# Decays in numbers of their own per slot, inputs scaled by a table of leads, and new tables for a four-layer image kernel

## The chip, the cores and the metric

The kernel runs on one core of one Trainium2 chip. The metric is device time in microseconds (us), from start to end of one execution. Times of a core's five engines are told apart: TensorE (PE, with its weight loads as PEld), VectorE (DVE), ScalarE (ACT), GpSimd (POOL), and SyncE (SP), which here only issues DMAs.

## The reference

The input is 32 images of 128 channels by 32 x 32 pixels, float32. Four layers are applied, each as `x = x + layer(group_norm(x))`:

1. a 3 x 3 convolution;
2. a 1 x 1 convolution, then a selective scan (Mamba) over the 1,024 pixels in four orders (forward and back, channels as they are and flipped), summed, and a second 1 x 1 convolution;
3. a gate of means over rows and columns, with two shorter selective scans;
4. a small simulated circuit on every pixel.

Nearly all time is layer 2. For each image and each of its four directions there are 256 inner channels (two halves `h` of 128) and 16 states `n`, and each state of each half is a recurrence along the 1,024 pixels:

```python
dA = jnp.exp(dt_t[..., None] * A)
h = dA * h + (dt_t * u_t)[..., None] * B_t[:, None, :]
y = jnp.einsum('bdn,bn->bd', h, C_t)
```

## The kernel before

Channels lie on the 128 partitions, pixels along the free dimension. The scans run in **slots**: one slot is one step `i`, that is one state `n` of one half `h` of one direction (`Direction`). A direction has 32 slots, an image 128, and the 32 images 4,096; layer 3 adds 64 more. `Steps.run` writes the instructions of slot `i` in one fixed order, and each engine works through its own queue in the order in which they were written; semaphores make it wait for data and for free buffers.

A step needs four things, made by different engines:

- the **decay** `da` (line 781): ScalarE's exponential of `dt` scaled by `A`, 128 x 1024. Before, slot `i` makes the decay of step `i + 3`;
- the **input** `bu`, 128 x 1024 in PSUM, made in one of two ways. A *plain* input: TensorE spreads row `B` over the partitions with two 512-column bf16 matmuls (line 802, in `spread`), and VectorE multiplies it by `du` in place (line 826, `input`). A *turned* input: `du` stands transposed in `dut`, pixels on the partitions, so that `B` is one number per partition; eight scalings of 128 x 128 write `but` (ScalarE, line 818, or as one instruction on GpSimd, line 815), and eight transposes on TensorE (line 795) bring it back into `bu`. `TURNED` says which of a direction's 32 slots are turned, `POOLED` which of these GpSimd scales;
- the **scan** (line 834): VectorE's `tensor_tensor_scan` over `da` and `bu`, into `hh`;
- the **weighing** (line 843): GpSimd multiplies `hh` by row `C`, spread over the partitions by a DMA (`cc`, line 772). Eight transposes on TensorE (line 879) then add it up in PSUM (`y`), and after 16 states ScalarE reads the sum (`evict`, line 898).

Before, slot `i` writes: `evict`, decay `i + 3`, ScalarE's waiting reads of PSUM (`flush`), `spread(i + 1)`, `scan(i)`, `input(i + 1)`, more reads, stages of other work, scaling of input `i + 4`, weighing `i`, sum of `i - 2`, load of `cc` for `i + 3`, and again stages.

The *stages* are all that is not the recurrence: convolutions (line 1131), projections (line 373: `uc`; 394, 485, 581), gates, transposes, statistics, the ways out. Where each stands is written in `PLACES`: for every kind of stage a slot relative to the direction's first, and a place within it (-1 is behind the slot's own work). `Table` carries this out. ScalarE reads the projections with silu and softplus, which need other activation tables than the decays' exponential: `Kernel.activation` (line 921) notes which table is in, a load is put ahead of it where the table changes, and `exps` (line 926) loads the exponential's table again before the next decay.

`Work.BUFS` gives the number of buffers in each ring of tiles. PSUM has two buffers for `bu`, two for all stages' matmuls (`mm`), and the sums `y`.

Of the kernel before, what the change touches and what calls it, by code (L numbers as in the profile page):

```python
# [41 lines left out]


TURNED = (
# [4 lines left out]
)  # L49

POOLED = (
    (5, 11, 21, 27),
    (7, 8, 13, 23, 24),
    (5, 12, 18, 22, 31),
    (7, 15, 19, 25),
)


# [1 line left out]
PLACES = {  # L60
    0: {
        "first": [
            (-41, -1), (-41, -1), (-38, -1), (-38, -1), (-35, 2), (-34, 0), (-32, 1), (-31, 2),
            (-28, 3), (-26, 3), (-25, 0), (-24, 2), (-23, 2), (-22, 3), (-18, 3), (-5, 2),
            (-3, 3), (-2, 2),
        ],
        "second": [
            (-8, 2), (-1, 0), (2, -1), (8, 1),
        ],
    },  # L70
    1: {
        "first": [
            (-48, 3), (-47, 3), (-46, 3), (-44, -1), (-39, 3), (-39, 3), (-38, 2), (-37, 2),
            (-33, 2), (-32, -1), (-31, -1), (-30, -1), (-29, 1), (-27, 0), (-25, 1), (-23, -1),
            (-13, 0), (-4, 0),
        ],
        "second": [
            (5, 3), (6, 2), (8, 3), (10, -1),
        ],
        "gates": [  # L80
            (1, -1), (3, 1), (6, -1), (17, -1),
        ],
        "back": [
            (21, 3), (26, 2),
        ],
        "out": [
            (39, -1), (47, 0), (52, -1), (54, 2),
        ],
    },
    2: {  # L90
        "first": [
            (-53, 2), (-52, 2), (-51, 1), (-48, 2), (-42, 0), (-40, -1), (-39, 3), (-37, 2),
            (-34, 2), (-33, 1), (-32, 0), (-31, 3), (-29, 3), (-28, 1), (-26, 1), (-15, 2),
            (-6, 3), (-1, -1),
        ],
        "second": [
            (-4, 2), (1, 2), (3, 2), (5, -1),
        ],
    },
    3: {  # L100
        "first": [
            (-53, 2), (-53, 2), (-51, 0), (-49, 1), (-45, 2), (-45, 3), (-44, 1), (-44, 3),
            (-40, 2), (-39, 3), (-36, 0), (-27, 1), (-23, 0), (-20, 1), (-18, -1), (-9, 3),
            (-8, 1), (-4, 2),
        ],
        "second": [
            (-15, -1), (-7, -1), (1, -1), (12, 0),
        ],
        "gates": [
            (-7, 2), (9, 1), (12, 0), (13, 0),  # L110
        ],
        "back": [
            (22, 3), (31, 3),
        ],
        "out": [
            (37, 2), (40, 3), (42, 1), (50, 3),
        ],
    },
    "layer0": [
        (-79, 3), (-76, 2), (-75, 2), (-73, -1), (-69, 0), (-64, 3), (-63, 2), (-62, 3),  # L120
        (-55, 3), (-54, -1), (-51, 1), (-50, 0), (-49, 2), (-47, 2), (-46, 0), (-43, 3),
        (-42, 0),
    ],
    "end": [
        (60, 3), (61, 3), (63, 1), (66, 0), (68, 0), (76, 2), (81, 3), (86, 1), (94, -1),
    ],
}


def constants():  # L130
# [565 lines left out]
class Steps:  # L696
# [3 lines left out]
    SLOTS = 2 * DS  # L700
# [3 lines left out]
        self.cc, self.da, self.hh, self.bu, self.but = {}, {}, {}, {}, {}  # L704
        self.sums = self.owed = None

    def run(self, ways, plan):

        k = self.k
        steps = [(w, h, n) for w in ways for h in range(2) for n in range(DS)]  # L710
        self.steps = steps
        for i in range(3):
            self.load(i)
        for i in range(3):
            self.decay(i)
# [55 lines left out]
        self.cc[i] = t = k.work.tile([P, w.T], F32, tag="cc", name="cc")  # L771
        k.nc.sync.dma_start(t, w.rows[n : n + 1].to_broadcast([P, w.T]))

    def decay(self, i):
        if not self.has(i):
            return
        k, (w, h, n) = self.k, self.steps[i]
        assert ("dt", h) in w.made
        self.da[i] = t = k.work.tile([P, w.T], F32, tag="da", name="da")
        k.exps()  # L780
        k.nc.scalar.activation(t, w.dt[h], AF.Exp, scale=w.m.na[:, h, n : n + 1])  # L781
        if w.segment:

            k.nc.gpsimd.memset(t[:, 0 :: w.segment], 0.0)
# [16 lines left out]
        for cs in w.chunks:  # L801
            k.nc.tensor.matmul(t[:, cs], k.sel[:, n], w.parts[:, cs], start=True, stop=True)  # L802

    def scale(self, i, engine):

        if not self.has(i) or not self.turned(i):
            return
        if (engine is self.k.nc.gpsimd) != self.pooled(i):
            return
        k, (w, h, n) = self.k, self.steps[i]  # L810
        assert "bt" in w.made and all(("dut", h, g) in w.made for g in range(w.T // P // 4))
        self.but[i] = t = k.work.tile([P, w.T // P, P], F32, tag="but", name="but")
        if self.pooled(i):
            each = w.bt[:, :, n : n + 1].to_broadcast([P, w.T // P, P])
            engine.tensor_tensor(t, w.dut[h], each, ALU.mult)  # L815
            return
        for b in range(w.T // P):
            engine.activation(t[:, b], w.dut[h][:, b], AF.Copy, scale=w.bt[:, b, n : n + 1])  # L818
# [82 lines left out]
class Kernel:  # L901
# [175 lines left out]
    def images(self):  # L1077
        tc, nc, d = self.tc, self.nc, self.d
        with ExitStack() as ctx:
# [179 lines left out]
            images, ways, plan = [], [], Table(self)  # L1259
# [460 lines left out]
```

## Time and profile before

| what | value |
|---|---|
| time, median of 3 runs | 12,785.62 us (12,782.69 to 12,790.93) |
| the profiled execution | 12,796.0 us, span 12,794.2 us |
| granted TensorE clock, mean | 0.983 |
| decays, line 781 | 4,096, mean 1,144 ns |
| scans, line 834 | 4,160, mean 2,274 ns |
| plain inputs' products, line 826 | 1,856, mean 1,212 ns |
| scalings of turned inputs on ScalarE, line 818 | 13,824, mean 392 ns |
| the same on GpSimd, line 815 | 576, mean 1,919 ns |
| table loads, lines 921 and 926 | 695 and 683, mean 1,283 ns |
| weighing, line 843 | 4,160, mean 2,373 ns |

A group's busy time is the union of its instructions' times, its mean the length of a single one; where instructions of an engine overlap in its pipeline, the mean is longer than the distance from one start to the next. The idle time of an engine is put down to the instruction that ended it. The 64 decays of layer 3 read other tiles and stand in groups of their own.

### The profile page before, as it was taken

Reading aid. Unit: us, or ns where it says so; the run is one execution under the profiler, and the core shown is the slowest. Engines: PE = TensorE matmul, PEld = TensorE weight load, DVE = VectorE, ACT = ScalarE, POOL = GpSimd, SP = SyncE. Lnnn points to the kernel's source line nnn. Section 1 sums busy time; section 2 is a strip of 40 time slices with the busy share of each in tenths; the row PEclk is TensorE's granted clock in tenths of the full one; section 3 lists DMA queues with packets and bytes.
Section 4 is the critical chain, followed back from the end, with each engine's and each line's share of the span. In section 5 each row is a group of like instructions: output and inputs, shape, how many; then the busy total and the mean of one; then the engine's idle time right before and its main releaser. Section 6 shows DMA issues by size and latency. Waiting matters only on the chain.

```text
span 12794.2 us, 209849 instructions
## 1 busy us (share of the span) xinstructions
PE 12351.5 (97%) x75694; PEld 8583.8 (67%) x75694; DVE 12186.0 (95%) x7817; ACT 12115.8 (95%) x22601; POOL 12040.9 (94%) x6421
## 2 busy tenths in 40 slices
PE   8999999999999999999999999999999999999888
PEld 5676676666666666766666666676666666667542
DVE  7999999999999999999999999999999999999876
ACT  7999999999999999999999999999999999999843
POOL 6999999999999999999999999999999999999865
PEclk9999999999999999999999999999999999999978
DMA  4555555555555555555555555555555555555432
GB/s 138 183 185 180 184 184 185 182 185 183 181 184 184 186 184 181 184 182 186 183 186 184 181 184 183 185 181 186 184 184 181 184 184 184 183 185 184 168 118 94
DMA packets 633943, 2278.38 MB, mean 178 GB/s; under 512 B 77480, under 2 KB 81144, under 8 KB 632776
## 3 DMA queue, kind: packets, MB, share of 16 engines
q1 hardware_dynamic: 630600, 2263.06, 50.9%
q8 instruction: 599, 9.81, 0.3%
q14 instruction: 440, 3.60, 0.1%
q10 hardware_dynamic: 2304, 1.90, 0.0%
HBM read 2221.35 MB, written 43.33 MB: 177 GB/s over the span
## 4 chain that ended last, share of the span: by engine, by line
PE 46%; ACT 39%; DVE 7%; issue 4%; POOL 3%; DMA 1%; DVEq 0%; SPq 0%; POOLq 0%; ACTq 0%
ACT da L781 14%; PE y L879 13%; ACT but L818 13%; PE mm L373 8%; PE bu L795 7%; DVE hh L834 5%; PE bu L802 4%; PE mm L1131 3%; ACT L926 3%; ACT L921 3%; POOL hh L843 2%; PE mm L394 2%; PE y L858 2%; PE mm L485 1%; DVE bu L826 1%
## 5 line engine op out<-in xcount | busy, mean ns | idle before, releaser
L843 POOL TENSOR_TENSOR hh<-hh,cc 128x1024 f32<-128x1024 f32 x4160 | 9768.1, 2373 | 371.2 <-DVE hh L834 188.8
L834 DVE TENSOR_TENSOR_SCAN hh<-da,bu 128x1024 f32<-128x1024 f32 x4160 | 9303.9, 2274 | 315.6 <-PE bu L795 55.3
L879 PEld LDWEIGHTS y<-cbig,hh 128*128 128x128 f32 x33280 | 3776.6, 142 | 1273.0 <-issue 977.6
L781 ACT ACTIVATE da<-dt,m_na 128x1024 f32<-128x1024 f32 x4096 | 4568.8, 1144 | 28.1 <-DVE hh L834 19.6
L879 PE MATMUL y<-cbig,hh 128*128 128x128 f32 x33280 | 4400.9, 276 | 71.7 <-POOL hh L843 67.2
L818 ACT ACTIVATE but<-dut,bt 128x128 f32<-128x128 f32 x13824 | 4216.4, 392 | 30.1 <-PE bu L795 30.1
L795 PE MATMUL bu<-cbig,but 128*128 128x128 f32 x18432 | 2413.6, 274 | 131.2 <-DVE hh L834 93.5
L826 DVE TENSOR_TENSOR bu<-du,bu 128x1024 f32<-128x1024 f32 x1856 | 2250.0, 1212 | 102.6 <-PE bu L802 91.9
L795 PEld LDWEIGHTS bu<-cbig,but 128*128 128x128 f32 x18432 | 2072.3, 141 | 323.9 <-issue 144.0
L373 PE MATMUL mm<-hpad,m_wc 128*128 128x512 f32 x4096 | 1937.2, 603 | 5.0 <-ACT dt L921 0.8
L373 PEld LDWEIGHTS mm<-hpad,m_wc 128*128 128x128 f32 x4096 | 712.2, 190 | 760.6 <-issue 688.5
L802 PE MATMUL bu<-parts,sel 48*128 48x512 bf16 x3712 | 1133.6, 386 | 64.8 <-DVE hh L834 55.4
L815 POOL TENSOR_TENSOR but<-dut,bt 128x1024 f32<-128x1024 f32 x576 | 1105.2, 1919 | 0.0
L921 ACT ACT_TABLE_LOAD x695 | 891.7, 1283 | 13.7 <-DMA my_zw<-in_my_zw 1.4
L926 ACT ACT_TABLE_LOAD x683 | 876.3, 1283 | 15.6 <-DMA cbig<-in_cbig 3.6
L501 POOL TENSOR_TENSOR du<-dt,uc 128x1024 f32<-128x1024 f32 x260 | 616.2, 2370 | 18.4 <-ACT dt L921 18.4
L858 PEld LDWEIGHTS y<-m_skip,uc 128*128 128x128 f32 x4096 | 488.5, 193 | 101.1 <-issue 55.4
L1131 PE MATMUL mm<-xpad,w 128*128 128x512 f32 x1152 | 542.9, 608 | 2.7 <-ACT xpad L1116 2.7
L802 PEld LDWEIGHTS <-sel 48*128 48x128 bf16 x3712 | 211.6, 94 | 489.4 <-issue 303.0
L858 PE MATMUL y<-m_skip,uc 128*128 128x128 f32 x4096 | 516.5, 280 | 0.5 <-ACT back L898 0.3
L394 PE MATMUL mm<-uc,m_xw 128*128 128x512 f32 x1024 | 494.7, 606 | 7.4 <-ACT dut L530 7.4
L921 ACT ACTIVATE uc<-mm,m_pv 128x512 f32<-128x512 f32 x512 | 335.0, 686 | 54.5 <-PE mm L373 47.3
(207 smaller groups left out, 7380.5 us busy)
## 6 DMA issues: line engine op xcount, KB each, us to landing
cc<-rows SPq DMA_DIRECT2D x4160, 512.0 KB, 3.9
xt<-in_x SPq DMA_DIRECT2D x32, 512.0 KB, 5.8
x<-xt SPq DMA_DIRECT2D x32, 512.0 KB, 3.3
xt<-x SPq DMA_DIRECT2D x32, 512.0 KB, 3.9
out<-xt SPq DMA_DIRECT2D x32, 512.0 KB, 2.9
rows<-dbl SPq DMA_DIRECT2D x130, 64.0 KB, 4.5
stats<-st SPq DMA_DIRECT2D x32, 36.0 KB, 3.0
means<-stats SPq DMA_DIRECT2D x1, 1152.0 KB
```

The source lines that it names most:

```text
L373: nc.tensor.matmul(self.view(ps), m.wc[:, v, j, h * P : (h + 1) * P], self.taps(j, c), start=(j == 0), stop=(j == 3),)
L781: k.nc.scalar.activation(t, w.dt[h], AF.Exp, scale=w.m.na[:, h, n : n + 1])
L795: k.nc.tensor.matmul(t[:, b * P : (b + 1) * P], but[:, b], k.ident, start=True, stop=True, is_transpose=True,)
L802: k.nc.tensor.matmul(t[:, cs], k.sel[:, n], w.parts[:, cs], start=True, stop=True)
L818: engine.activation(t[:, b], w.dut[h][:, b], AF.Copy, scale=w.bt[:, b, n : n + 1])
L826: k.nc.vector.tensor_tensor(t, w.du[h], t, ALU.mult)
L834: k.nc.vector.tensor_tensor_scan(way(t), way(self.da.pop(i)), way(self.bu.pop(i)), 0.0, ALU.mult, ALU.add)
L843: k.nc.gpsimd.tensor_tensor(t, t, self.cc.pop(i), ALU.mult)
L858: nc.tensor.matmul(self.y[g][: w.bl, b], w.uc[h][:, at], m.skip[:, h], start=(b == 0), stop=False)
L879: k.nc.tensor.matmul(self.y[g][: w.bl, b], t[:, at], k.ident, start=False, stop=(n == DS - 1 and b == w.per - 1), is_transpose=True,)
L921: self.nc.scalar.activation(*args, **kw)
L926: self.nc.scalar.preload_act_table_set("natural_log_exp_and_others")
```

## The change

- **Decays.** `decay` no longer takes a step's number. It makes the next decay in line, and a new table `DECAYS` of 128 numbers says how many decays each slot of an image writes: 0, 1, 2 or 3. Three are made before the first slot, as before.
- **Scaling.** A turned input is no longer scaled four slots ahead of its step, but as many as the new table `LEADS` says for it, 2 to 7 (0 stands for plain inputs). `scale` looks from slot `i` at the steps up to eight ahead and scales those whose lead fits, first ScalarE's, then, after the weighing, GpSimd's.
- **Rings.** `da` has six buffers instead of five, `but` four instead of three.
- **Kinds of inputs.** `TURNED` has 75 entries in place of 72, `POOLED` 17 in place of 18.
- **Slots.** All numbers in `PLACES` are others; the stages are the same.

Layer 3 runs with one decay a slot and a lead of four throughout (the defaults of `run`).

```diff
--- before.py
+++ after.py
@@ -42,17 +42,17 @@
 
 
 TURNED = (
-    (4, 5, 6, 8, 9, 11, 13, 15, 16, 17, 19, 21, 22, 23, 25, 27, 28, 30),
-    (1, 2, 4, 7, 8, 10, 11, 13, 15, 16, 18, 22, 23, 24, 26, 28, 29, 30, 31),
-    (4, 5, 6, 7, 8, 11, 12, 13, 15, 16, 17, 18, 21, 22, 26, 28, 30, 31),
-    (1, 3, 5, 7, 8, 10, 11, 13, 15, 19, 21, 22, 23, 25, 29, 30, 31),
+    (2, 3, 5, 7, 9, 11, 12, 14, 16, 17, 19, 20, 22, 23, 25, 27, 29, 31),
+    (0, 2, 5, 7, 9, 11, 12, 13, 14, 16, 17, 18, 22, 23, 25, 27, 28, 29, 30, 31),
+    (4, 5, 6, 7, 8, 9, 11, 14, 15, 16, 18, 20, 21, 23, 24, 27, 30, 31),
+    (0, 2, 3, 6, 7, 9, 11, 12, 13, 14, 19, 20, 21, 22, 24, 27, 29, 30, 31),
 )
 
 POOLED = (
-    (5, 11, 21, 27),
-    (7, 8, 13, 23, 24),
-    (5, 12, 18, 22, 31),
-    (7, 15, 19, 25),
+    (7, 14, 23, 29),
+    (2, 12, 17, 22, 29),
+    (4, 15, 31),
+    (6, 9, 20, 21, 30),
 )
 
 
...
@@ -60,71 +60,94 @@
 PLACES = {
     0: {
         "first": [
-            (-41, -1), (-41, -1), (-38, -1), (-38, -1), (-35, 2), (-34, 0), (-32, 1), (-31, 2),
+            (-39, 1), (-39, 2), (-37, 3), (-36, -1), (-33, 2), (-31, -1), (-28, 0), (-28, 2),
...
+DECAYS = (
+    0, 1, 0, 1, 3, 0, 0, 1, 1, 2, 1, 2, 0, 0, 2, 1, 1, 1, 1, 2, 0, 2, 1, 1, 0, 2, 1, 1, 0, 0, 2, 2,
+    1, 0, 0, 0, 2, 2, 0, 1, 0, 2, 1, 1, 1, 1, 1, 3, 0, 0, 0, 2, 3, 0, 1, 0, 0, 2, 3, 0, 3, 0, 0, 2,
+    1, 2, 1, 0, 0, 1, 1, 0, 0, 1, 3, 3, 0, 1, 3, 1, 0, 2, 0, 0, 1, 0, 2, 0, 1, 2, 0, 1, 3, 0, 0, 1,
+    2, 0, 2, 0, 2, 3, 0, 0, 0, 0, 2, 1, 0, 2, 3, 0, 3, 0, 0, 0, 1, 2, 0, 0, 3, 1, 2, 1, 0, 2, 0, 1,
+)
+
+LEADS = (
+    (
+        0, 0, 2, 3, 0, 5, 0, 5, 0, 5, 0, 7, 5, 0, 7, 0, 5, 6, 0, 5, 5, 0, 3, 6, 0, 3, 0, 5, 0, 7, 0, 4,
+    ),
+    (
+        5, 0, 7, 0, 0, 5, 0, 7, 0, 4, 0, 5, 6, 4, 2, 0, 4, 7, 3, 0, 0, 0, 5, 7, 0, 6, 0, 7, 6, 6, 4, 4,
+    ),
+    (
+        0, 0, 0, 0, 5, 5, 6, 5, 5, 3, 0, 5, 0, 0, 5, 4, 3, 0, 5, 0, 7, 3, 0, 4, 6, 0, 0, 2, 0, 0, 5, 5,
+    ),
+    (
+        6, 0, 3, 2, 0, 0, 7, 5, 0, 7, 0, 3, 7, 5, 3, 0, 0, 0, 0, 4, 6, 4, 5, 0, 2, 0, 0, 7, 0, 2, 4, 4,
+    ),
+)
 
 
 def constants():
@@ -254,8 +277,8 @@
 
 
     BUFS = {
-        "uc": 4, "dt": 3, "du": 3, "dut": 2, "parts": 2, "dbl": 2, "cc": 3, "da": 5, "hh": 4,
-        "bt": 2, "but": 3,
+        "uc": 4, "dt": 3, "du": 3, "dut": 2, "parts": 2, "dbl": 2, "cc": 3, "da": 6, "hh": 4,
+        "bt": 2, "but": 4,
     }
 
     def __init__(self, pool):
@@ -704,20 +727,24 @@
         self.cc, self.da, self.hh, self.bu, self.but = {}, {}, {}, {}, {}
         self.sums = self.owed = None
 
-    def run(self, ways, plan):
+    def run(self, ways, plan, decays=(1,), leads=((4,) * SLOTS,)):
+
+
 
         k = self.k
+        self.leads, self.next = leads, 0
         steps = [(w, h, n) for w in ways for h in range(2) for n in range(DS)]
         self.steps = steps
         for i in range(3):
             self.load(i)
         for i in range(3):
-            self.decay(i)
+            self.decay()
         self.spread(0)
         self.input(0)
         for i in range(len(steps) + 2):
             self.evict()
-            self.decay(i + 3)
+            for _ in range(decays[i % len(decays)]):
+                self.decay()
             k.flush(False, vector=False)
             self.spread(i + 1)
             self.catch_up()
@@ -726,9 +753,9 @@
             k.flush(False)
             if self.has(i):
                 plan.slot(i, self.load_of(i))
-            self.scale(i + 4, k.nc.scalar)
+            self.scale(i, k.nc.scalar)
             self.weigh(i)
-            self.scale(i + 4, k.nc.gpsimd)
+            self.scale(i, k.nc.gpsimd)
             self.add(i - 2)
             self.load(i + 3)
             if self.has(i):
@@ -771,7 +798,9 @@
         self.cc[i] = t = k.work.tile([P, w.T], F32, tag="cc", name="cc")
         k.nc.sync.dma_start(t, w.rows[n : n + 1].to_broadcast([P, w.T]))
 
-    def decay(self, i):
+    def decay(self):
+
+        i, self.next = self.next, self.next + 1
         if not self.has(i):
             return
         k, (w, h, n) = self.k, self.steps[i]
@@ -801,12 +830,16 @@
         for cs in w.chunks:
             k.nc.tensor.matmul(t[:, cs], k.sel[:, n], w.parts[:, cs], start=True, stop=True)
 
-    def scale(self, i, engine):
-
-        if not self.has(i) or not self.turned(i):
-            return
-        if (engine is self.k.nc.gpsimd) != self.pooled(i):
-            return
+    def scale(self, slot, engine):
+
+        for i in range(slot + 1, slot + 9):
+            if not self.has(i) or not self.turned(i):
+                continue
+            lead = self.leads[i // self.SLOTS % len(self.leads)][i % self.SLOTS]
+            if i - slot == lead and (engine is self.k.nc.gpsimd) == self.pooled(i):
+                self.scaled(i, engine)
+
+    def scaled(self, i, engine):
         k, (w, h, n) = self.k, self.steps[i]
         assert "bt" in w.made and all(("dut", h, g) in w.made for g in range(w.T // P // 4))
         self.but[i] = t = k.work.tile([P, w.T // P, P], F32, tag="but", name="but")
@@ -1297,7 +1330,7 @@
                 plan.alone(PLACES[0]["first"][0][0])
                 self.circuit(Slices(self.work.tile([P, 2 * HW], F32, tag="carry", name="small")))
                 plan.alone(0)
-                Steps(self).run(ways, plan)
+                Steps(self).run(ways, plan, DECAYS, LEADS)
                 plan.alone()
```

More of the change, by code (lines that the diff above doesn't have):

```diff
@@ L62 @@
         "first": [
[L63 to L65 removed]
+            (-39, 1), (-39, 2), (-37, 3), (-36, -1), (-33, 2), (-31, -1), (-28, 0), (-28, 2),
+            (-24, 2), (-22, 3), (-21, 0), (-20, 3), (-18, 0), (-15, 2), (-11, 2), (-9, 3),
+            (-4, 3), (-3, 0),
         ],
         "second": [
[L68 removed]
+            (-10, 0), (0, 1), (3, 1), (6, 0),
         ],
@@ L72 @@
         "first": [
-            (-48, 3), (-47, 3), (-46, 3), (-44, -1), (-39, 3), (-39, 3), (-38, 2), (-37, 2),
-            (-33, 2), (-32, -1), (-31, -1), (-30, -1), (-29, 1), (-27, 0), (-25, 1), (-23, -1),
-            (-13, 0), (-4, 0),
+            (-50, 1), (-50, 3), (-49, -1), (-48, 3), (-40, 1), (-39, 0), (-38, -1), (-37, -1),
+            (-32, 1), (-31, -1), (-29, 3), (-27, 1), (-26, 3), (-25, 0), (-24, 2), (-20, -1),
+            (-15, 0), (-14, 3),
         ],
         "second": [
-            (5, 3), (6, 2), (8, 3), (10, -1),
+            (4, 2), (5, 2), (6, 2), (8, 0),
         ],
         "gates": [
-            (1, -1), (3, 1), (6, -1), (17, -1),
+            (-1, 0), (0, -1), (1, 1), (2, 2),
         ],
         "back": [
-            (21, 3), (26, 2),
+            (26, 1), (30, 1),
         ],
         "out": [
-            (39, -1), (47, 0), (52, -1), (54, 2),
+            (40, 3), (42, 0), (50, 0), (53, 2),
         ],
@@ L91 @@
         "first": [
-            (-53, 2), (-52, 2), (-51, 1), (-48, 2), (-42, 0), (-40, -1), (-39, 3), (-37, 2),
-            (-34, 2), (-33, 1), (-32, 0), (-31, 3), (-29, 3), (-28, 1), (-26, 1), (-15, 2),
-            (-6, 3), (-1, -1),
+            (-55, 3), (-53, 2), (-51, 3), (-50, 2), (-44, 1), (-42, 0), (-40, 2), (-39, 2),
+            (-37, 2), (-35, 0), (-34, 3), (-33, 1), (-31, 3), (-30, 3), (-27, 1), (-11, 2),
+            (-10, -1), (-9, 1),
         ],
         "second": [
-            (-4, 2), (1, 2), (3, 2), (5, -1),
+            (-4, 2), (0, 0), (4, 2), (6, 0),
         ],
@@ L101 @@
         "first": [
-            (-53, 2), (-53, 2), (-51, 0), (-49, 1), (-45, 2), (-45, 3), (-44, 1), (-44, 3),
-            (-40, 2), (-39, 3), (-36, 0), (-27, 1), (-23, 0), (-20, 1), (-18, -1), (-9, 3),
-            (-8, 1), (-4, 2),
+            (-56, 2), (-55, 0), (-54, -1), (-50, 2), (-45, -1), (-45, -1), (-44, -1),
+            (-44, -1), (-40, 3), (-39, 2), (-27, 2), (-25, 3), (-20, -1), (-18, -1), (-16, 1),
+            (-15, 2), (-11, 0), (-7, 1),
         ],
         "second": [
-            (-15, -1), (-7, -1), (1, -1), (12, 0),
+            (-15, -1), (-8, 1), (-3, 2), (12, -1),
         ],
         "gates": [
-            (-7, 2), (9, 1), (12, 0), (13, 0),
+            (-3, 0), (6, 1), (7, 1), (18, 2),
         ],
         "back": [
-            (22, 3), (31, 3),
+            (30, -1), (31, 3),
         ],
         "out": [
-            (37, 2), (40, 3), (42, 1), (50, 3),
+            (35, 3), (36, 2), (38, 3), (48, 0),
         ],
@@ L119 @@
     "layer0": [
-        (-79, 3), (-76, 2), (-75, 2), (-73, -1), (-69, 0), (-64, 3), (-63, 2), (-62, 3),
-        (-55, 3), (-54, -1), (-51, 1), (-50, 0), (-49, 2), (-47, 2), (-46, 0), (-43, 3),
-        (-42, 0),
+        (-78, 0), (-76, 0), (-72, -1), (-70, 2), (-67, 3), (-65, 0), (-63, 0), (-62, 0),
+        (-55, 3), (-53, 2), (-51, 0), (-48, 3), (-46, 1), (-45, -1), (-44, 3), (-43, -1),
+        (-40, 1),
     ],
     "end": [
-        (60, 3), (61, 3), (63, 1), (66, 0), (68, 0), (76, 2), (81, 3), (86, 1), (94, -1),
+        (58, 0), (62, 2), (66, 2), (69, 0), (71, 3), (82, 0), (97, 1), (114, -1), (118, 1),
     ],
 }
+DECAYS = (
[4 rows of a table added]
+)
[13 more added lines that the diff above has]
+)
 def constants():
```

## The prediction

> **What bounds the kernel now.** I read the page's busy times first, then the stretch view to see whether one stage stands for the whole, then the groups of a long steady stretch, then what VectorE waits for, and last the order of time in a few microseconds, since busy times of pipelined engines flatter them.
>
> ```profile
> span 12794.2 us, 209849 instructions
> PE 12351.5 (97%) x75694; PEld 8583.8 (67%) x75694; DVE 12186.0 (95%) x7817; ACT 12115.8 (95%) x22601; POOL 12040.9 (94%) x6421
> ```
>
> ```profile
> core 0: us, PE busy (x) PEld busy (x) DVE busy (x) ACT busy (x) POOL busy (x), PEclk, DMA share, GB/s
> 4000.00:4400.00 400.00, 392.15 (x2465) 277.60 (x2464) 389.45 (x240) 395.07 (x740) 389.73 (x208) 1.00 0.53 184
> ```
>
> The span is one long steady stage, about 11,900 us at a granted clock of 1.00, with a short end. Four engines are busy 97 to 99% in it at once, so a stage is worth what the tightest of the four gives back. The groups from 2,000 to 10,000 us (line, engine, out<-in, shape, count | busy, mean ns | idle before):
>
> ```profile
> L834 DVE TENSOR_TENSOR_SCAN hh<-da,bu 128x1024 f32<-128x1024 f32 x2729 | 6100.9, 2274 | 200.1 <-PE bu L795 36.2 <-PE y L879 12.8 <-PE mm L1005 11.9
> L826 DVE TENSOR_TENSOR bu<-du,bu 128x1024 f32<-128x1024 f32 x1193 | 1446.5, 1212 | 18.3 <-PE bu L802 11.2
> L781 ACT ACTIVATE da<-dt,m_na 128x1024 f32<-128x1024 f32 x2729 | 3044.3, 1144 | 10.7 <-DVE hh L834 5.3
> L818 ACT ACTIVATE but<-dut,bt 128x128 f32<-128x128 f32 x9216 | 2811.0, 392 | 19.8 <-PE bu L795 19.8
> L921 ACT ACT_TABLE_LOAD x447 | 573.5, 1283 | 7.9
> L926 ACT ACT_TABLE_LOAD x447 | 573.5, 1283 | 7.9
> L843 POOL TENSOR_TENSOR hh<-hh,cc 128x1024 f32<-128x1024 f32 x2730 | 6410.1, 2374 | 194.3 <-DVE hh L834 107.5 <-DMA cc<-rows 32.4 <-PE mm L581 16.3
> ```
>
> 2729 scans in 8,000 us are 2.931 us a slot, or 375.2 us an image of 128 slots. What each engine needs of that I take from start to start of neighbouring instructions in the trace (the lower quartile for each kind of pair, times how often the pair stands in an image):
>
> ```profile
> 5999.68 2.26 DVE L834 TENSOR_TENSOR_SCAN hh<-da,bu 128x1024 f32<-128x1024 f32 x1
> 6001.86 1.21 DVE L826 TENSOR_TENSOR bu<-du,bu 128x1024 f32<-128x1024 f32 x1
> 6001.99 1.13 ACT L781 ACTIVATE da<-dt,m_na 128x1024 f32<-128x1024 f32 x1
> 6003.15 1.28 ACT L921 ACT_TABLE_LOAD   x1
> 6003.19 2.29 DVE L834 TENSOR_TENSOR_SCAN hh<-da,bu 128x1024 f32<-128x1024 f32 x1
> ```
>
> A scan takes 2.18 us to the next start. An input product (L826) takes 1.34 when its own scan follows at once, because that scan must wait for it, and 1.115 when something else stands between. So in an image VectorE needs 367.8 us for itself, ScalarE 368.2, GpSimd 363.9. TensorE's 98% is not what it needs: its records overlap. In the chain of waits from 6,000 us
>
> ```profile
> 6000.14 0.54 PE bu L802 x2
> 6005.14 0.87 PE bu L795 x8
> ```
>
> eight transposes follow each other in 0.87 us (0.109 each), and summed so TensorE needs 351 us. VectorE then waits, from 1,000 to 11,500 us (28 images):
>
> ```profile
> DVE hh L834 <- PE bu L795: 47.2, 112, 0.7
> DVE hh L834 <- PE y L879: 17.1, 28, 0.6
> DVE hh L834 <- PE mm L1005: 16.0, 28, 0.6
> DVE bu L826 <- PE bu L802: 14.9, 54, 0.6
> DVE hh L834 <- ACT but L818: 11.0, 5, 2.7
> ```
>
> With the small rows it is 119 us, 4.2 an image; 3.2 more is scatter in the durations. VectorE is the bound (367.8 of 375.2 its own work), ScalarE stands just as full beside it, and what VectorE still waits for is mostly TensorE arriving late after a burst of other matmuls. One thing speaks against this: the page's chain is 46% TensorE and only 7% VectorE. That chain follows an in-order queue back through whatever stood before, so I trust the sums of own work.
>
> **The change part by part.** The instruction lists of the two programs differ in seven kinds only (with the weight loads at L802).
>
> *Table loads.* 1,378 loads at L921 and L926 become 938: 440 fewer, 13.75 an image. Decays need the exponential table; slots without a decay let several silu and softplus reads pass between two loads. The load's row says 1.283 us, and in the excerpt the decay before it is lengthened: 1.16 from its start to the load against 1.04 to another activation. The return costs as much, so a load costs 1.283 + 0.13 = 1.41 us and ScalarE is given 19.4 us an image. The Trainium skill ("ScalarE: Activation LUTs", What ACT_TABLE_LOAD costs) agrees on 1283 ns but adds a drain of 1380 ns, 2.66 us a switch; by it the saving were 36.6 us. The trace shows 0.13 of that drain, so I take 19.4.
>
> *Inputs.* Per image 72 turned inputs become 75, so 53 products instead of 56 on VectorE. GpSimd scales 17 instead of 18, ScalarE 58 instead of 54. ScalarE: 32 more activations at 0.292 from start to start, +9.3. GpSimd: one product of 1.919 less, -1.9. TensorE: three times eight transposes at 0.109 for two matmuls of 0.54 in all, 3 x 0.33 = +1.0. The skill speaks against this part: "TensorE: Matmul & The Clock Gate", Part 4, gives about 275 ns for a turned 128x128 in a kernel. The trace's mean of one at L795 is 274 ns, the same number, but the next starts 109 ns later; at 275 each the three would cost 3 x (2.2 - 0.54) = +5 us an image, still inside TensorE's 24 us of room. VectorE: three products less; of the rest 36 instead of 43 are followed at once by their scan. Summed over all neighbouring pairs, 367.8 becomes 363.6: -4.2. (Three products at 1.34 are 4.0, the same size.)
>
> *Sum by engine, an image:* VectorE 363.6, GpSimd 362.0, ScalarE 368.2 - 19.4 + 9.3 = about 358, TensorE 352. VectorE stays the bound.
>
> *Decays in other numbers.* A slot now issues 0 to 3 decays (52, 37, 26, 13 slots of 128). Before, a decay was always issued three slots ahead of its scan. Now six are issued in the scan's own slot (36, 41, 51, 57, 73, 74), 25 one ahead, 42 two, 37 three, 13 four, 5 five. Before, a decay ended 7.2 us before its scan (median; 1.7 at least). Three slots are 8.8 us, so with ScalarE at the same place in time those six would end 1.6 us late. Queued behind a late decay is all of ScalarE: reads of PSUM (two buffers, so TensorE waits for them), scalings. Behind the late scan stand GpSimd's weighing, the load of cc on SP that waits for it, and TensorE's spread two slots on. Bounds: nothing, or a little gain, if ScalarE runs ahead; 6 x 1.6 = 9.6 us an image if it keeps its place. Before most of these slots its queue is light. For slot 41, the work of slots 38 to 41 up to that decay is about 7.3 us against 8.8 of time; for 51, 5.7 of 8.8; for 57, 6.8 of 8.8. Slot 36 is tight: a table load, two scalings and reads in slots 32 to 35 make 13.7 us of 11.7. I take 1 us an image.
>
> *Three decays in a row* stand ahead of the slot's reads of PSUM: 3.1 us instead of 1.04, so a bank is freed up to 2.1 us later. TensorE's 23 us of room covers it; if it did not, it would come back as "PE mm" and "PE bu" waits. *Rings:* da six instead of five, but four instead of three. Decay j waits for scan j-6; that scan was issued at least one slot before. I cost both at nothing: they only take space. *Scaling leads* of 2 to 7 slots instead of 4: a scaling waits for the spread that frees its buffer; in 24 of about 370 that spread is of the same slot, before in 20 of 357, so the same. *Places:* the same stages in other slots; reads on ScalarE are grouped, the number of DMAs on SP is unchanged, and cc's loads keep their place at the end of a slot. SP waits for GpSimd nearly all the time, so another DMA queued there waits at most one slot, and each has several slots of lead. Four-matmul bursts in one slot (uc) are five instead of six an image. I take -1 us of waits for the fewer bursts and the freed ScalarE (TensorE waited about 2 us an image for it).
>
> *Sum:* -4.2 + 1 - 1 = -4.2 us an image, times 32 is -134 us. Head and end keep their stages: nothing. The profiled execution, 12,796.0 us (span 12,794.2 and 1.8 around it), lies 10 above the median of 12,785.6, so the forecast for the median is 12,785.6 - 134 = 12,651, said as 12,650.
>
> **The rivals.**
>
> *Waits go too (14%).* VectorE waits fall from 4.2 towards nothing because ScalarE has 10 us less: 363.6 + 3.2 = 366.8 an image, -8.4 x 32 = 12,517. For: two engines were equally full, now one is. Against: only 11 us of the 119 are named ScalarE's; the rest is TensorE's order.
>
> *GpSimd becomes the bound (10%).* It needs 362.0 and now stands idle 11.3; if that idleness stays, 373.3 an image, -61 us: 12,725. Against: most of it is waiting for the scan (140 us of some 250), which shortens with VectorE.
>
> *Little changes (5%).* New waits of about 4 an image eat the gain: within 25 us of 12,786.
>
> *Short decays (13%), slower.* ScalarE does not run ahead, since its reads of PSUM and its scalings hang on TensorE's slot, and the six decays end 1.6 us late: +9.6 - 4.2 = +5.4 an image, +173 us: 12,960. It decides from 0.7 us each. For: the 7.2 us. Against: ScalarE's 10 us of room, and that scan i-5 had ended 4.0 us (median) before its buffer was taken, so it may start earlier.
>
> **How the numbers follow.** The sum as it stands has 58%, with 12,600 to 12,700 of its own (1.5 us an image either way). Faster: 58 + 14 + 10 = 82%; same 5%; slower 13%. 0.2%, 25 us, is about what a measurement of this kernel tells from no change. The range of 8 in 10 leaves out the slower case (13%) and the lower half of the case without waits (7%): 12,555 to 12,790.
>
> **What would show it.** ScalarE's busy time 12,115.8 - 440 x 1.283 + 1,024 x 0.305 = 11,864; VectorE 12,186.0 - 96 x 1.212 = 12,070; GpSimd 11,980. Scans every 2.90 us. VectorE's waits still name TensorE, 3 to 5 us an image; waits of the scan on "ACT da" at most 1 or 2. ScalarE below 97% of a steady stretch. Wrong would be: a row "DVE hh <- ACT da" of over 4 us an image, at the six slots named; VectorE's products at the old price with the slot unchanged; or TensorE's own spacing above 0.109 us.

## Result and the profile after

The changed kernel takes 12,635.69 us (median of 4 runs, 12,625.21 to 12,644.96); the kernel before, on the same chip, 12,788.28 us. The ratio is 0.9879 (95% interval 0.9867 to 0.9892), 153 us or 1.2% less. The forecast was 12,650.

The page of the changed kernel. VectorE is `DVE`; its lines have moved: the scan is L867, the product L859, the decay L810, ScalarE's scaling L851, GpSimd's weighing L876, the table loads L954 and L959, the sum L912, the transposes into `bu` L824, the spread L831.

```profile
span 12634.7 us, 210848 instructions
PE 12298.3 (97%) x76270; PEld 8670.6 (69%) x76270; DVE 12047.9 (95%) x7721; ACT 11814.3 (94%) x23185; POOL 11971.2 (95%) x6389
```

The stretch from 4,000 to 4,400 us, with the columns of the prediction's row for the kernel before:

```profile
4000.00:4400.00 400.00, 395.71 (x2531) 286.91 (x2530) 388.19 (x234) 387.94 (x779) 389.34 (x206) 0.99 0.54 187
```

ScalarE fell from 395.07 busy of 400 to 387.94. VectorE and GpSimd kept their share of a shorter time. The groups from 2,000 to 10,000 us:

```profile
L867 DVE TENSOR_TENSOR_SCAN hh<-da,bu 128x1024 f32<-128x1024 f32 x2763 | 6167.0, 2272 | 183.6 <-PE y L912 46.1 <-PE bu L824 26.5 <-POOL hh L876 3.9
L859 DVE TENSOR_TENSOR bu<-du,bu 128x1024 f32<-128x1024 f32 x1143 | 1382.5, 1210 | 24.0 <-PE bu L831 18.2
L810 ACT ACTIVATE da<-dt,m_na 128x1024 f32<-128x1024 f32 x2763 | 3000.6, 1143 | 17.2 <-DVE hh L867 13.6
L851 ACT ACTIVATE but<-dut,bt 128x128 f32<-128x128 f32 x10022 | 3021.3, 394 | 49.9 <-PE bu L824 49.9
L959 ACT ACT_TABLE_LOAD x302 | 387.5, 1283 | 5.3
L954 ACT ACT_TABLE_LOAD x301 | 386.2, 1283 | 5.1
L876 POOL TENSOR_TENSOR hh<-hh,cc 128x1024 f32<-128x1024 f32 x2763 | 6481.4, 2373 | 114.6 <-DVE hh L867 70.2 <-DMA cc<-rows 19.2 <-PE bu L824 8.9
```

2763 scans in the same time, 2.895 us a slot in place of 2.931. Single instructions cost what they did: only their numbers differ. ScalarE's idle time before its scalings rose to 49.9 us; it now waits for others.

In the trace's order of time a product followed by its scan still takes 1.34 us from start to start (3885.78 to 3887.12):

```profile
3885.78 1.21 DVE L859 TENSOR_TENSOR bu<-du,bu 128x1024 f32<-128x1024 f32 x1
3887.12 4.46 DVE L867 TENSOR_TENSOR_SCAN hh<-da,bu 128x1024 f32<-128x1024 f32 x2
```

What VectorE waits for, from 1,000 to 11,500 us:

```profile
DVE hh L867 <- PE y L912: 60.0, 108, 1.6
DVE hh L867 <- PE bu L824: 34.7, 100, 0.9
DVE bu L859 <- PE bu L831: 23.7, 85, 0.5
DVE hh L867 <- ACT da L810: 0.5, 1, 0.5
```

These are TensorE's lateness still, 133 us with the small rows in 28.3 images, 4.7 an image (4.2 before). Decays are not waited for: one wait of 0.5 us in the whole stretch.

By the starts of the scans of images 3 to 30, an image takes 370.58 us, 4.72 less than before (375.30). I sorted that time by what VectorE does between two starts. Products took 72.54 us an image and now take 67.72: 4.82 less. All from scan to next start is 0.74 less, everything else 0.83 more. So nearly the whole gain lies in the time of the products: three fewer at 1.34 (4.0), and four more of the rest have other VectorE work behind them, so that their scan need not wait for them (4 x 0.225 = 0.9).

TensorE's granted clock (column `PEclk`, 1.00 in full) is not quite the same in both kernels. In both traces it falls to 0.50 for stretches of 3.4 us, at times two on end. In images 3 to 30 such stretches make 1.6 us an image before and 3.4 us after, where they stand in slots 37, 38 and 82. The same instructions are slower in them: the four matmuls of L1224 in slot 82 take 1.98 us together in images 5 and 9, and 3.0 to 3.6 us in the seven others of images 3 to 11, in which the clock falls in slot 82. Slots 82 and 83 together are 1.68 us longer in the 13 images with such a stretch in slot 82 than in the 15 without. Images with no stretch at 0.50 take 374.72 us before (21 of 28) and 369.49 us after (10 of 28), 5.2 us less. So about half a microsecond an image of what the change gives is lost again to the clock. What starts a stretch is not shown: in the changed kernel none follows within 6 us of a wait of TensorE over 0.7 us, while in a run below (no lead over four) 22 of 27 waits of 3.0 to 3.5 us are followed by one.

### The profile page after: what moved, and what is told of

It is laid out like the page before. It is cut to its first block, busy times and chain, and to the rows that moved or that the text cites. A ratio compares the mean times of both kernels' runs of the same rounds, so it can differ in the third digit from the quotient of the medians.

```text
span 12634.7 us, 210848 instructions
## 1 busy us (share of the span) xinstructions
PE 12298.3 (97%) x76270; PEld 8670.6 (69%) x76270; DVE 12047.9 (95%) x7721; ACT 11814.3 (94%) x23185; POOL 11971.2 (95%) x6389
## 4 chain that ended last, share of the span: by engine, by line
PE 69%; ACT 17%; DVE 8%; issue 3%; POOL 3%; DMA 0%; DVEq 0%; SPq 0%; POOLq 0%; ACTq 0%
PE y L912 20%; PE bu L824 12%; PE mm L396 11%; ACT da L810 6%; PE bu L831 5%; ACT but L851 5%; DVE hh L867 5%; PE mm L417 4%; PE mm L1164 4%; PE y L891 3%; POOL hh L876 2%; PE mm L577 2%; PE mm L604 2%; PE mm L546 2%; ACT L954 2%
## 5 line engine op out<-in xcount | busy, mean ns | idle before, releaser
L876 POOL TENSOR_TENSOR hh<-hh,cc 128x1024 f32<-128x1024 f32 x4160 | 9758.6, 2373 | 253.4 <-DVE hh L867 134.2
L867 DVE TENSOR_TENSOR_SCAN hh<-da,bu 128x1024 f32<-128x1024 f32 x4160 | 9288.0, 2272 | 292.5 <-PE y L912 67.5
L912 PEld LDWEIGHTS y<-cbig,hh 128*128 128x128 f32 x33280 | 3777.7, 141 | 1175.4 <-issue 985.7
L851 ACT ACTIVATE but<-dut,bt 128x128 f32<-128x128 f32 x14848 | 4476.2, 393 | 71.9 <-PE bu L824 71.7
L810 ACT ACTIVATE da<-dt,m_na 128x1024 f32<-128x1024 f32 x4096 | 4447.8, 1142 | 27.9 <-DVE hh L867 22.6
L912 PE MATMUL y<-cbig,hh 128*128 128x128 f32 x33280 | 4381.1, 276 | 58.1 <-POOL hh L876 57.4
L824 PE MATMUL bu<-cbig,but 128*128 128x128 f32 x19200 | 2524.1, 275 | 27.5 <-DVE hh L867 20.1
L824 PEld LDWEIGHTS bu<-cbig,but 128*128 128x128 f32 x19200 | 2183.3, 141 | 214.2 <-issue 127.9
L859 DVE TENSOR_TENSOR bu<-du,bu 128x1024 f32<-128x1024 f32 x1760 | 2128.6, 1209 | 97.7 <-PE bu L831 88.9
L396 PE MATMUL mm<-hpad,m_wc 128*128 128x512 f32 x4096 | 1943.4, 603 | 34.6 <-ACT dt L954 23.5
L396 PEld LDWEIGHTS mm<-hpad,m_wc 128*128 128x128 f32 x4096 | 709.4, 190 | 776.9 <-issue 694.3
L831 PE MATMUL bu<-parts,sel 48*128 48x512 bf16 x3520 | 1075.6, 386 | 66.0 <-DVE hh L867 65.2
L848 POOL TENSOR_TENSOR but<-dut,bt 128x1024 f32<-128x1024 f32 x544 | 1043.6, 1918 | 0.0
L891 PEld LDWEIGHTS y<-m_skip,uc 128*128 128x128 f32 x4096 | 488.5, 194 | 49.9 <-issue 23.6
L831 PEld LDWEIGHTS <-sel 48*128 48x128 bf16 x3520 | 196.5, 94 | 440.1 <-issue 290.6
L954 ACT ACTIVATE uc<-mm,m_pv 128x512 f32<-128x512 f32 x512 | 334.8, 685 | 108.5 <-PE mm L396 105.5
```

What stands on the lines that cost most here:

```text
L396: nc.tensor.matmul(self.view(ps), m.wc[:, v, j, h * P : (h + 1) * P], self.taps(j, c), start=(j == 0), stop=(j == 3),)
L824: k.nc.tensor.matmul(t[:, b * P : (b + 1) * P], but[:, b], k.ident, start=True, stop=True, is_transpose=True,)
L859: k.nc.vector.tensor_tensor(t, w.du[h], t, ALU.mult)
L867: k.nc.vector.tensor_tensor_scan(way(t), way(self.da.pop(i)), way(self.bu.pop(i)), 0.0, ALU.mult, ALU.add)
L876: k.nc.gpsimd.tensor_tensor(t, t, self.cc.pop(i), ALU.mult)
L891: nc.tensor.matmul(self.y[g][: w.bl, b], w.uc[h][:, at], m.skip[:, h], start=(b == 0), stop=False)
```

## The experiments

All are compared with the kernel before on the same chip. Where I give a difference by slot, it is between the starts of the scans, averaged over images 3 to 30. Theory 1 is that VectorE's own work is the bound and that ScalarE's saved time only pays for more turned inputs. Theory 2: the saved table loads are the gain. Theory 3: the new places and leads are.

**Three turned inputs made plain again** in the changed kernel.

```diff
 TURNED = (
-    (2, 3, 5, 7, 9, 11, 12, 14, 16, ...
+    (2, 3, 5, 7, 9, 11, 14, 16, ...
-    (0, 2, 5, 7, 9, 11, 12, 13, 14, 16, ...
+    (0, 2, 5, 7, 9, 11, 12, 14, 16, ...
...
-    (0, 2, 3, 6, 7, 9, 11, 12, 13, 14, 19, ...
+    (0, 2, 3, 6, 7, 9, 11, 13, 14, 19, ...
```

> The changed kernel with three of its 75 turned inputs an image plain again (slots 12, 45 and 108 of the image), all else kept: VectorE gets 96 products back, ScalarE loses 24 scalings an image (7 us). Theory 1 (VectorE's own work is the bound, and ScalarE's saved table loads only paid for turning three more inputs): about +4 us an image, +128, near 12,765. Theory 2 (the gain is ScalarE's time: fewer table loads mean fewer waits on it): ScalarE has still more room, so no slower than the changed kernel, 12,636 or a little under. Theory 3 (the new slots and leads made TensorE's bursts lighter): also about 12,636.

12,717.71 us, ratio 0.9943 (0.9928 to 0.9958). Three slots, 11, 44 and 107, each just ahead of a changed one, became longer by 1.34 us each: the product, exactly. 1.65 us came back elsewhere. Of this, 1.04 stands in slots 38, 82 and 83, where TensorE's clock fell 28 times in the 28 images of the changed kernel; here it falls in 7 images, and never in slot 82. For the rest, ScalarE and TensorE had less to do, which may be the reason. VectorE's largest wait went down (60.0 us in the changed kernel):

```profile
DVE hh L867 <- PE y L912: 36.9, 89, 0.6
```

So 2.37 us an image, half the gain, is the net of turning three inputs. (Images without a stretch at half clock take 372.80 us here and 369.49 in the changed kernel: 3.3 us.) Theory 2 falls as an account of this half: ScalarE had still more room here and the kernel was slower. So does theory 3: places and leads stayed. The other 2.35 us an image are there with as many products as before (56). Of these the products' time is 1.09 (four more of them are covered by other VectorE work) and the scans' waits and durations 1.56, less 0.29 that VectorE's other work takes more.

**The decays' table alone,** on the kernel before, and **three more turned inputs alone,** and **both**.

```diff
+DECAYS = (
...
+    1, 1, 1, 1, 2, 0, 0, 2, 1, 1, 1, 1, 1, 1, 1, 1, 2, 0, 0, 2, 1, 1, 1, 1, 1, 1, 1, 1, 1, 1, 1, 1,
...
-            self.decay(i + 3)
+            for _ in range(decays[i % len(decays)]):
+                self.decay()
-        "da": 5
+        "da": 6
```

```diff
-    (4, 5, 6, 8, 9, 11, 13, 15, 16, 17, 19, ...
+    (4, 5, 6, 8, 9, 11, 13, 15, 16, 17, 18, 19, ...
...
-    ... 15, 16, 17, 18, 21, 22, 26, 28, 30, 31),
+    ... 15, 16, 17, 18, 21, 22, 24, 26, 28, 30, 31),
-    (1, 3, 5, 7, 8, 10, 11, 13, 15, 19, ...
+    (1, 3, 5, 7, 8, 10, 11, 13, 15, 17, 19, ...
```

> The kernel before with decays in numbers of their own (0 to 3 a slot, by a table made for its old slots, da ring of six): 284 table loads fewer, 8.9 an image, so ScalarE is given about 12.5 us an image; inputs, leads and places as before. Theory 1: VectorE's own work is the same, so at most the waits that hang on ScalarE go: 0 to -2 us an image, 12,725 to 12,788. Theory 2: most of the gain, 12,640 to 12,690. Theory 3: none, 12,788.

> The kernel before with three more turned inputs an image (slots 18, 88 and 113), scaled by ScalarE four slots ahead, table loads as before: VectorE loses 96 products, ScalarE gets 24 scalings an image, 368 + 7 = 375 us of 375. Theory 1: ScalarE takes VectorE's place as the bound, 375 plus its waits of 7: 0 to +7 us an image, 12,790 to 13,000. Theory 2: slower too, +7 us an image, 13,010. If products alone decided: -4 an image, 12,660.

> Both parts on the kernel before: the table of decays (284 loads fewer) and three more turned inputs, with the old places, a lead of four and three but buffers. ScalarE 368.2 - 12.5 + 7.0 = 362.7 us an image, VectorE 363.8. Theory 1: the whole gain comes back without new places and leads, -4 us an image, about 12,660. Theory 2: as ScalarE's net relief of 5.5 us of 12.5: 12,720. Theory 3 (places and leads carry it): about 12,788 or slower.

| run | us | ratio (95%) |
|---|---|---|
| table of decays alone | 12,871.52 | 1.0060 (1.0043 to 1.0077) |
| three more turned alone | 13,006.05 | 1.0167 (1.0152 to 1.0183) |
| both | 13,103.72 | 1.0243 (1.0227 to 1.0258) |

The second run came out where theory 2 had it and 6 us past the end of theory 1's range, but the third shows that a full ScalarE was not the reason: with the table as well, ScalarE is busy 378.59 of 400 us and scans are late behind the same slots (19, 88, 111 and 115). The first no theory foretold; of the third, theory 3 alone had said "or slower", with no size. Saving 284 table loads made the kernel slower, and the two parts together were worse than each alone. Theory 2 is out; theory 1 as I had put it fails too, since own work is not enough. The run with the table shows the price of late decays: slot 83, where silu reads and a reload end, makes three decays, and the decay of step 84 ended 0.1 us before its scan on average, where it had ended 9.6 us before it; that scan came 1.0 us later. Of the 2.9 us by which an image is longer here, another 1.14 goes with TensorE's clock at slot 39: it falls just ahead of that slot in 21 of 28 images (in 6 before), and where it does not, slot 39 takes 2.2 us in both kernels. The waits of the run with the table alone:

```profile
DVE hh L845 <- PE bu L806: 71.4, 97, 2.7
DVE hh L845 <- ACT da L792: 35.4, 31, 2.7
```

The second row was 0.7 us before. In the run with three more turned inputs, the trace shows what an extra scaling does (image 10, slots 109 to 112; start, duration, engine, line):

```profile
4248.71 2.45 ACT L818 ACTIVATE but<-dut,bt 128x128 f32<-128x128 f32 x8
4253.51 1.08 ACT L921 ACTIVATE sz<-mm 128x512 f32<-128x512 f32 x2
4254.16 1.61 PE L485 MATMUL mm<-dbl,m_dw 32*128 32x512 f32 x4 [2.42 <-ACT sz L921]
4257.05 1.03 PE L802 MATMUL bu<-parts,sel 48*128 48x512 bf16 x2
4258.12 1.23 DVE L826 TENSOR_TENSOR bu<-du,bu 128x1024 f32<-128x1024 f32 x1 [3.41 <-PE bu L802]
```

The scaling (2.45 us) stands in ScalarE's queue ahead of the silu reads of `mm`. TensorE wants a bank for L485 and waits 2.42 us for the read that frees one. Behind L485 in its queue stands the spread L802, and behind that VectorE's product, 3.41 us late. A part of the 3.41 is TensorE's clock, at 0.50 for 3.4 us from 4256.32: the spread takes 1.03 us, and had taken 0.60 at 4248.24. That ScalarE need not be full for this, the run with both parts shows. I call it theory 1a: *ScalarE ahead of a read, a bank, the spread, the scan.*

**Three other turned inputs, then a fourth buffer.** The two parts again, with slots chosen so that no read seemed to follow (turned: 26, 78, 123); then the same with `but` of four.

> As the run with both parts on the kernel before, but the three more turned inputs are others (slots 26, 78 and 123), whose scalings on ScalarE stand four slots ahead where no read of PSUM by ScalarE follows within a slot or two; table of decays as in the run with that alone (12,872). Theory 1a (a scaling in front of a read holds one of TensorE's two PSUM banks, the spread behind comes late, VectorE's product waits; where the scaling stands decides): the products' 4 us an image come off, 12,872 - 128 = 12,745. Rival (a fourth turned input near others always stalls at a lead of four and three buffers, wherever it stands): about 13,000 to 13,100 as before.

> The run with three turned inputs at slots 26, 78 and 123 on the kernel before (13,174), with four but buffers instead of three. There ScalarE waited up to 3.1 us for TensorE to free a buffer, inside the run of eight turned slots 75 to 82, and scans 80 and 81 came 6 us an image late. Theory 1b (with three buffers at a lead of four, a run of turned slots ties ScalarE to TensorE's spread, and the reads queued behind it come late): the 6 us at slot 80 go, 12,980. If the wait for the buffer is only where lateness from elsewhere shows: 13,150 to 13,175.

13,173.53 us (ratio 1.0301, 1.0285 to 1.0316), and with the fourth buffer 13,052.39 us (1.0202, 1.0185 to 1.0219). My choice of slots was bad: the products went (slots 25 and 77 are 1.34 us shorter), but, against the run with the table alone, scans behind slot 80 came 6.05 us and those behind slot 122 3.54 us late. At slot 80 the first cause was the ring: a run of eight turned slots at a lead of four asks for a buffer that the spread of the same slot frees. A fourth buffer took 3.71 us of the 6.05 off, and changed no other slot by more than 0.13. At slot 122 TensorE's L381 waited for a softplus read (72.0 us in 27 waits), theory 1a again. The time is above both ranges of the first expectation, and each of its readings has one of the two slots. The ring gave 3.8 of the 6 us an image that I expected of it.

**One decay a slot** in the changed kernel (`run(ways, plan, (1,), LEADS)`), and **no lead over four** (`min(lead, 4)`, which moves 47 of 75 scalings up to three slots later).

> The changed kernel with one decay in each slot as before (always three ahead), all other tables kept: the reads are placed so that every silu or softplus is now followed by a reload, 566 table loads more, 17.7 an image. ScalarE 357.6 + 17.7 x 1.41 = 382.6 us an image of 370.6. Theory 1 (VectorE bound, ScalarE's time is the price that pays for the turned inputs): ScalarE becomes the bound, at least 12 us an image slower than the changed kernel, with its waits up to 19: 13,020 to 13,250. Rival (the numbers of decays are beside the point, places and leads carry the gain): 12,640 to 12,700.

> The changed kernel with every lead above four cut to four (47 of 75; shorter ones kept): the same work, scalings up to three slots later. Theory 1a: some scalings now stand in front of reads of PSUM or end just before their spread: slower by 1 to 6 us an image, 12,670 to 12,830. If leads only give room that is not used: 12,636.

13,812.17 us (ratio 1.0801, 1.0785 to 1.0817) and 13,309.83 us (1.0407, 1.0389 to 1.0424): 37 and 21 us an image over the changed kernel, both above what I expected. With one decay a slot ScalarE is not even full (378.31 of 400 us), and TensorE's clock is 0.95 in the mean:

```profile
4000.00:4400.00 400.00, 371.70 (x2285) 265.58 (x2284) 355.58 (x212) 378.31 (x720) 355.79 (x189) 0.95 0.49 168
```

On average, the scans behind slots 35, 107 and 119 come 7.0 to 9.4 us later than in the changed kernel. Of 407.8 us an image TensorE spends 38.7 at half clock, where it had spent 3.4 of 370.6; if it had work all that time, that is up to 17.7 of the 37 us (an estimate, half of the difference). TensorE's longest waits in this run are for ScalarE's silu and softplus reads, as in theory 1a, but how much of the 37 us each link brings was not told apart. The run with short leads has the cleanest view of one such place. First the changed kernel around slot 8 of image 10, then the same place with short leads:

```profile
3831.54 4.45 DVE L867 TENSOR_TENSOR_SCAN hh<-da,bu 128x1024 f32<-128x1024 f32 x2
3834.68 1.09 ACT L954 ACTIVATE dt<-mm 128x512 f32<-128x512 f32 x2
3835.32 1.98 PE L396 MATMUL mm<-hpad,m_wc 128*128 128x512 f32 x4 [0.75 <-ACT dt L954]
3837.15 1.03 PE L912 MATMUL y<-cbig,hh 128*128 128x128 f32 x8
3837.25 6.64 DVE L867 TENSOR_TENSOR_SCAN hh<-da,bu 128x1024 f32<-128x1024 f32 x3
```

```profile
4037.76 2.45 ACT L851 ACTIVATE but<-dut,bt 128x128 f32<-128x128 f32 x8
4038.12 4.45 DVE L867 TENSOR_TENSOR_SCAN hh<-da,bu 128x1024 f32<-128x1024 f32 x2
4043.60 1.09 ACT L954 ACTIVATE dt<-mm 128x512 f32<-128x512 f32 x2
4044.25 2.91 PE L396 MATMUL mm<-hpad,m_wc 128*128 128x512 f32 x4 [3.10 <-ACT dt L954]
4046.95 1.83 PE L912 MATMUL y<-cbig,hh 128*128 128x128 f32 x8
4049.80 4.46 DVE L867 TENSOR_TENSOR_SCAN hh<-da,bu 128x1024 f32<-128x1024 f32 x2 [3.68 <-PE bu L824]
```

From the first scan to the softplus read it is 3.14 us in the changed kernel, 5.48 with short leads: later by 2.34, the time of eight scalings. TensorE's wait for the read grows from 0.75 to 3.10, by the same 2.35, and a scan behind it, which had run on without a wait, waits 3.68. The last step is larger than the others because TensorE's clock is at 0.50 from 4045.16 to 4048.58: four matmuls of L396 take 2.91 us instead of 1.98, eight of L912 1.83 instead of 1.03. From the start of the read to the end of the eight transposes that the scan waits for (L824) it is 4.38 us in the changed kernel and 6.06 here, 1.68 more. So 2.34 us of scalings and 1.68 us of clock make the scan's input 4.0 us later, of which the scan waits 3.68. Theory 1a holds here link by link, with the clock as a link that it had not named.

It is not the whole of this run. By the waits from 1,000 to 11,500 us, scans wait longest for decays:

```profile
DVE hh L867 <- ACT da L810: 234.9, 170, 3.3
DVE hh L867 <- PE bu L824: 192.7, 109, 3.7
DVE hh L867 <- ACT but L851: 109.5, 94, 3.7
```

The first row was 0.5 us in the changed kernel. Behind a later scaling, a decay in ScalarE's own queue comes late and holds the scan with no PSUM bank in between.

**The rings as before,** each alone, in the changed kernel (`"but": 3`; `"da": 5`).

> The changed kernel with three but buffers as before instead of four, leads and all else kept. Theory 1b: scalings seven slots ahead must wait for a buffer, and ScalarE's reads behind them come late: slower by 3 to 20 us an image, 12,730 to 13,280. If the ring only takes space, as the prediction put it: 12,636.

> The changed kernel with five da buffers as before instead of six. Five decays an image are five slots ahead and thirteen four, and must now wait for the scan just started or just before: ScalarE is held up to 3 us at these places. Theory 1b: 1 to 5 us an image slower, 12,670 to 12,800. If the ring only takes space, as the prediction put it: 12,636.

13,120.99 us (ratio 1.0256, 1.0240 to 1.0271) and 13,054.68 us (1.0204, 1.0189 to 1.0219), 15 and 13 us an image over the changed kernel; the first within what I expected, the second far above. With three scaling buffers ScalarE's scalings wait 466.0 us for TensorE from 1,000 to 11,500 us (64.4 in the changed kernel), and the scans' longest wait is again for decays (173.7 us). With five decay buffers the scan behind slot 82 alone comes 6.8 us late. A decay is made five slots ahead there, and its buffer is free only when the scan just ahead ends:

```profile
4173.18 1.15 ACT L810 ACTIVATE da<-dt,m_na 128x1024 f32<-128x1024 f32 x1 [3.56 <-DVE hh L867]
4175.64 1.08 ACT L954 ACTIVATE dt<-mm 128x512 f32<-128x512 f32 x2
4176.28 2.56 PE L508 MATMUL mm<-dbl,m_dw 32*128 32x512 f32 x4 [4.20 <-ACT dt L954]
4179.84 1.23 DVE L859 TENSOR_TENSOR bu<-du,bu 128x1024 f32<-128x1024 f32 x1 [4.52 <-PE bu L831]
```

The same chain, begun by a buffer, and again with the clock in it: it is at 0.50 for 10.2 us from 4174.65, and the four matmuls of L508 take 2.56 us.

**More turned inputs** in the changed kernel: two (slots 81 and 104), and one (slot 28, a lead of four).

```diff
-    (..., 25, 27, 29, 31),
+    (..., 25, 27, 28, 29, 31),
...
-        ..., 0, 5, 0, 7, 0, 4,
+        ..., 0, 5, 4, 7, 0, 4,
```

> The changed kernel with two more turned inputs an image (slots 81 and 104, leads of five, scaled in slots 76 and 99 where ScalarE has nothing else): VectorE 363.6 - 2.7 = 360.9 us an image, ScalarE 357.6 + 4.7 = 362.3, GpSimd 362.0 unchanged. Theory 1 (VectorE's own work still bounds): -2.7 us an image, 12,550. If GpSimd or ScalarE is as near as the sums say: half of it or none, 12,590 to 12,640. If the scalings disturb reads: slower.

> The changed kernel with one more turned input an image (slot 28, a lead of four: scaled in slot 24, where ScalarE has no other work and no read follows before slot 26; a buffer is free by then). Theory 1: VectorE's product of 1.34 us goes, -1.3 us an image, 12,593, if nothing else binds. If the balance of the four engines is such that GpSimd or TensorE now stands in its place, or a read comes late: 12,620 to 12,700.

12,792.81 us (ratio 1.0002, 0.9993 to 1.0010) and 12,669.69 us (0.9903, 0.9888 to 0.9917). Neither beats the changed kernel. With two, one scaling waited 1.94 us for a `but` buffer ahead of a read, and the scan behind slot 81 came 3.7 us late; TensorE's clock fell in that slot in each of the 28 images. With one, slot 27 is 1.34 us shorter as expected, but slot 28 is 1.19 longer and slot 35 0.87. In slot 28 it is no late read:

```profile
3897.09 1.88 PE L409 MATMUL mm<-uc,m_xw 128*128 128x512 f32 x4
3899.68 1.04 PE L816 MATMUL bu<-cbig,but 128*128 128x128 f32 x8
3900.85 2.29 DVE L859 TENSOR_TENSOR_SCAN hh<-da,bu 128x1024 f32<-128x1024 f32 x1 [1.13 <-PE bu L816]
```

The clock is at 1.00 here. TensorE has a projection (L409), a sum and the transposes (L816) to do while one scan runs, and without the product VectorE is merely back sooner to wait for it. Where TensorE's work between two scans is longer than a scan's 2.18 us, the product had been hidden. Slot 35 was not looked into.

## Why the prediction was right

**The bound.** VectorE's own work as the bound was right, and shown: a product put back costs 1.34 us in its slot, three times out of three. The other way, a product less pays only where TensorE is not late in the same place, as the run with one more turned input shows. The page's chain (now 69% TensorE) was rightly not taken for it.

**VectorE's term, -4.2 an image.** The products' time fell by 4.8. I had read the counts (three fewer, 36 instead of 43 followed at once), but let the sum over all pairs stand, which the other pairs' small changes had brought down to 4.2. This is the largest part of the 18 us that the forecast was short.

**Table loads.** 440 fewer, as counted. ScalarE's busy time was put at 11,864 us and is 11,814.3: decays that now follow each other overlap in its pipeline, so their group's busy time fell by 121 us (4,568.8 to 4,447.8). The sum had left that out; other overlaps must have gone the other way, and were not told apart. That the saved time is no gain in itself the run with the table alone shows; that these tables need it, the run with one decay a slot (with the clock's part in that).

**Short decays, +1.** Measured: one wait of 0.5 us in 28 images. The decays of the six slots ended 0.3 to 2.0 us before their scans on average: the margin was thin, and ScalarE did run ahead, as the light queues before these slots had suggested, slot 36 (0.5 us) included. The rival had its mechanism right, as the 0.1 us margin at slot 84 in the run with the table alone shows, but not this kernel's place for it.

**Waits, -1.** They did not fall. VectorE's rose from 4.2 to 4.7 an image. In images without a stretch at half clock they are 3.7 in both kernels, so the rise goes with TensorE's clock, for which the prediction has no term. The freed ScalarE was worth less than I gave it. This error and the one for short decays have opposite signs and nearly cancelled, and the clock took back about 0.5 us an image of a gain that was larger than forecast. That the number came within 15 us of the measured time owes this much to luck; the main term does not.

**Rings and leads "at nothing".** As steps of this change they cost nothing. But I said that they only take space, and that was wrong: taking one of them back costs 13 to 21 us an image. They are what keeps reads and decays early enough. That three decays in a row or a late read are covered by TensorE's 23 us of room was the wrong reason too: its room is a mean over the image, and the run with short leads shows a delay of 2.35 us at one bank passed on to the scan in full, with 1.68 us of slower clock on top.

**Rivals.** Waits did not go, GpSimd did not become the bound (its idle time ahead of the weighing fell from 194.3 to 114.6 us), and new waits did not eat the gain.

What stays open: how the 2.35 us an image that are not the three inputs divide between places, leads and decays. Each of these taken back alone costs about three to eight times the whole gain, so they can't be summed. Of the 1.65 us that three more turned inputs bring elsewhere, 1.04 stands where TensorE's clock falls; ScalarE's and TensorE's parts in the rest were not told apart. And no run holds the clock fixed, so its part in the slower runs is known only at the places shown.

## What to carry to other kernels

When four engines are 97% busy, the own work of the tightest one gives the size of a gain, but whether it comes is decided at single places: ask of each instruction that you add to a queue what stands behind it, and which small ring (here two PSUM banks) it keeps closed. A saved table load or a lighter engine was worth nothing by itself here; it was worth what could be moved onto that engine without standing in front of a read or a decay. Read TensorE's granted clock beside each delay before you put the whole of it down to a queue. Tables of orders, leads and rings that were made together should be judged together: each part alone, either way, was slower here.

## What was unexpected of the hardware

A delay of 2.3 us on an engine with spare time (in the run with short leads ScalarE is busy 92% of a steady stretch, 368.81 of 400 us) reached TensorE undiminished (2.34 us of scalings, 2.35 of TensorE's added wait), and on the way to the scan it grew by 1.68 us, since TensorE's clock then stood at half for 3.4 us. One more buffer of one tile was worth 15 us an image in the changed kernel, and 3.8 in the kernel before with both parts. And one kernel's images differ by their clock alone: in the kernel before, 22 images have no fall of the clock just ahead of slot 39, and in the six that have one (6.8 us at 0.50) that slot is 2.7 us longer.
